# Group norm and quantised 3x3 convolution on one core: fewer plain images, no additions by hand in the middle, earlier input stores, a new timetable

## The chip, the core and the metric

The kernel runs on one core of one Trainium2 chip. The time is the device time of one execution in microseconds (us), and it is given as the median of several runs. A profile is one execution of its own, recorded by the hardware profiler; its times are read against that execution's time.

The core has five engines that run side by side, each with its own queue of instructions which it works off strictly in order: TensorE (PE, matrix products; its weight loads are listed as PEld), VectorE (DVE), ScalarE (ACT), GpSimd (POOL) and SyncE (SP), which here only issues DMAs. POOL issues DMAs too. 16 DMA engines carry the transfers of both queues. An instruction that needs another engine's result waits for a semaphore, and everything behind it on its own engine waits with it.

## What is computed

The input is 160 images of 128 channels and 32x32 pixels, with five sets of weights. Images are numbered here in the kernel's order, 32 per set.

```python
beta = jnp.max(U); alpha = jnp.min(U)
s1 = (beta - alpha) / 3.0
v1 = s1 * floor(U / s1)
s2 = s1 / 5.0
v2 = s2 * floor((U - v1) / s2)
w = (v1 + v2).reshape(128 * 5, 128, 3, 3)
...
x = x + conv3x3(group_norm(x, 32 groups), w)     # five groups, padding 1
```

So each image gets statistics (mean and variance of groups of four channels), is normalised, is convolved with its set's 3x3 weights, and the raw image is added to the result. The weights are quantised in two steps over the range of all five sets.

## The kernel before, in words

**Tiling.** The channels lie on the 128 partitions, an image is 1024 values of each. Two neighbouring images are a chunk; ten chunk places in SBUF hold loaded images (`CHUNKS`). A load brings a chunk (1 MB). A chunk's place can be loaded again once everything that reads its images is done.

**Two ways to convolve an image.** Both split the normalised image in a high and a low fp16 part, and PE multiplies both.

- A *plain* image (those in `PLAIN`, 33 of them) is normalised by POOL (`normalise_beside`, L858), ACT rounds it to the high part `hi` (L787), DVE subtracts for the low part `lo` (L894), and PE runs nine taps on two halves for two parts: 36 matmuls (L931).
- A *combined* image (120 of them) goes through sums and differences of pixels first. POOL (`differences`, L819 and L852) and DVE (`combine`, L831 and L838) write four quarters `v`; ACT scales and rounds them to `vh` (L881); DVE makes the rest `vl` (L887). PE then needs 24 matmuls (L986): six for each of two sums `m1` and `m2`, twelve for the two halves of the result. Between them ACT takes `m2` out of PSUM (`leave`, L1023), and DVE writes half the sum and half the difference of `m1` and `m2` into the two result banks (`pairs`, L1032 and L1034).

The images 0 to 6 are handled in ways of their own, which the change leaves alone.

**The result and the residual.** An image that is added *by hand* (`by_hand`: the first three, the last four and those in `HANDS`) is added to the raw image by DVE straight from PSUM (`residual`, L1075), and SP stores the sum (L1087); until then the image keeps its chunk place. For all others SP stores the raw image to the output early (`store_input`, L1094 for a whole chunk, L1087 for one image), ACT copies the result from PSUM to one of three `sum` buffers (the evacuation, L1058), and POOL issues a DMA that adds the buffer to what lies in the output (`accumulate`, L1081). That DMA waits for the store of the raw image, and the buffer is free when it has landed.

**Statistics.** Images are measured in groups of five. For most, ACT reads an image twice (`measure`: sum L377, squares L384); PE averages over channels; small instructions of DVE (L432 to L445), ACT (L415) and POOL (L422, a power) make `ngm`, `rstd`, `shift`.

**Weights.** While images of one set are convolved, the next set's weights are quantised in 42 small steps, most on DVE.

**What sets the order.** The first part (`run`) is written out by hand, with loads of chunks 1 to 9 ahead. From image 3 on (`steady`) the order on every queue is planned on the host by `Timetable`: each piece of work is a job with an engine, a cost in us, needs and a due time that is worked back from PE's list. `HASTE` moves due times by kind, `MARGIN` adds time after other engines' results, `SOON` says how long an engine is held free for an urgent job. Jobs with the engine "beside" are POOL's; they are placed beside `window` jobs of DVE (`pairs` and additions by hand), and then wait for DVE to get there. Stores and loads of SP are jobs of an endless queue with an assumed 14 us to landing. The plan fixes the order alone: on the chip each engine runs its list and waits where something is late.

Of the kernel before, what the change touches and what calls it, by code (L numbers as in the profile page):

```python
# [46 lines left out]
class Timetable:  # L47
# [6 lines left out]
    HOP = 0.14  # L54
    HASTE = {"combine": 5.0, "vh": -1.0, "vl": 1.0, "z": -5.0, "lo": 2.0, "sum": -3.0, "ve": -1.0, "power": -1.0, "scale": 2.0, "step": 1.0, "taps": -6.0, "across": 4.0}
    MARGIN = {"vh": 0.3, "pairs": 0.15, "hand": 0.45, "evac": 0.3, "t": 0.45}
    SOON = 0.6
    EARLY = 5.0
# [462 lines left out]
class Main:  # L521
# [24 lines left out]
    CHUNKS = 10  # L546
    LANDING = 14.0
    WIDE, HIGHS, ROWS, SUMS = 3, 4, 4, 3
    STEADY = 7
    BY_VECTOR = (8, 10, 11, 14, 19, 24, 29, 34)  # L550
    PLAIN = (9, 13, 17, *(22 + 9 * k + d for k in range(15) for d in (0, 4)))
    Z_ENGINE = "beside"
    HANDS = range(24, 156, 10)
    EARLY = 8
# [544 lines left out]
    def run(self):  # L1099
        nc, P = self.nc, self.P  # L1100
# [127 lines left out]
        for c in range(6, self.CHUNKS):  # L1228
            self.load(c)
        for i in range(self.FIRST):  # L1230
            j = (i - 1) % self.FIRST
            if i == self.FIRST - 1:
                for which in (1, 0):
                    self.sum_of_pairs(self.FIRST, which)
            self.direct_hi(j, self.COLS[2])
            self.direct_lo(j, self.COLS[2])
            if i == 0:
                self.stats[2].variances()
                self.stats[2].deviation()
                self.stats[2].power()  # L1240
                self.stats[2].scales()
                run(self.sums_across(0, nc.gpsimd))
                measure(0, 8, 9, 10)
            if i == 1:
                self.normalise(4)
                self.high_part(4)
            if i == 2:
                self.load_set(1)
                self.leave(3)
                self.normalise(5)  # L1250
                measure(1, 9)
                self.high_part(5)
                self.pairs(3)
                measure(0, 11)
                self.low_part(4)
                run(self.combinations(4))
            self.residual(j)
        self.steady(12, self.CHUNKS)

    def steady(self, measured, loaded):  # L1260
# [41 lines left out]
        for i in images:  # L1302
            comb, plain = self.combined(i), self.plain(i)
            if comb:
                beside[i] = add("t", "beside", 1.41, lambda i=i: self.differences(i))
                wide[i] = add("combine", "vector", 1.73, lambda i=i: self.combine(i))
                high[i] = add("vh", "scalar", 1.89, lambda i=i: self.high_combined(i), (beside[i], wide[i]))
                low[i] = add("vl", "vector", 2.28, lambda i=i: last_of(self.low_combined(i)), (high[i],))
            else:
# [21 lines left out]
            if i < imgs - 1:  # L1331
                out[i] = add("hand" if hand else "evac", "vector" if hand else "scalar", 1.15 if hand else 0.96, result, (main[i][1],))
                out[i].window = hand
            else:
                out[i] = add("hand", "vector", 2.0, result, (main[i][1],))
# [11 lines left out]
        for c in range(imgs // NB):  # L1347
            both, before = (range(k * NB, k * NB + NB) for k in (c, c - self.CHUNKS))
            if c >= loaded:
                loads[c] = add("load", "queue", self.LANDING, lambda c=c: self.load(c), (  # L1350
                    [stores.get(c - self.CHUNKS), *(j for i in before for j in readers(i))]
                ))
            if not all(self.by_hand(i) for i in both):
                stores[c] = add(
                    "store", "queue", self.LANDING, lambda c=c: self.store_input(c),
                    (loads.get(c), loads.get(c + 1)), ready=6.0 * c if c < loaded else 0.0,
                )
            for i in both:
                if not self.by_hand(i):
                    whole[i].after(stores[c])  # L1360

# [38 lines left out]
        for g, group in enumerate(self.groups):  # L1400
# [3 lines left out]
            for i in group:  # L1404
# [3 lines left out]
                if self.by_vector(i):  # L1408
# [3 lines left out]
                    continue  # L1412
                one = add("sum", "scalar", 1.06, lambda i=i: self.measure(i, (0,)), (load,))
                two = add("square", "scalar", 1.16, lambda i=i: self.measure(i, (1,)), (one,))
                measuring.append(two)
# [5 lines left out]
            ve = add("ve", "scalar", 0.16, lambda st=st: st.deviation(), (var,))  # L1421
            power = add("power", "beside", 0.4, lambda st=st: [st.power()], (ve,))
            scale = add("scale", "vector", 0.3, lambda st=st: st.scales_by_vector(), (power,))
            last_ve, last_dev = ve, dev
# [10 lines left out]
        for n in range(1, N_SETS):  # L1435
# [6 lines left out]
            for col in self.COLS:  # L1442
                gen = self.make_column(n, col, "later")
                for kind, cost in (
                    ("scalar", 0.7), ("vector", 0.74), ("vector", 0.56), ("vector", 0.56),
                    ("vector", 0.48), ("vector", 0.28), ("vector", 0.68), ("scalar", 0.5),
                    ("vector", 0.56), ("vector", 0.56), ("vector", 0.56), ("vector", 0.48),
                    ("vector", 0.28), ("vector", 0.5),
                ):
                    steps.append((kind, cost, gen))  # L1450
            taps = []
            for k, (kind, cost, gen) in enumerate(steps):
# [9 lines left out]
                if k % 14 == 13:  # L1462
# [3 lines left out]
                    taps.append(turned)  # L1466
            across = add("across", "vector", 0.9, lambda n=n: run(self.sums_across(n, nc.vector)), taps)
            for i in range(use, min(use + 3, imgs)):
# [66 lines left out]
```

## Time and profile before

| | before |
|---|---|
| median of 3 runs | 989.24 us (988.69 to 991.32) |
| the profiled execution, its own time | 988.58 us |
| its span, first to last instruction | 986.9 us |
| mean granted TensorE clock | 0.995 |
| PE, DVE, ACT, POOL busy | 937.3, 916.7, 854.2, 518.1 us |
| transfers | 246.88 MB, mean 250 GB/s |

The profile's page gives each engine's busy time; a table by stretches gives it for any part of the span, with the granted clock and the share of time in which the 16 DMA engines were moving packets (its highest value over ten microseconds is 1.05 in this trace). The waits list who idled for whom. A line such as L887 is a line of the kernel before; in the changed kernel, lines behind the first added one are one to four lines further down.

### The profile page before, as it was taken

Reading aid. Unit: us, or ns where it says so; the run is one execution under the profiler, and the core shown is the slowest. Engines: PE = TensorE matmul, PEld = TensorE weight load, DVE = VectorE, ACT = ScalarE, POOL = GpSimd, SP = SyncE. Lnnn points to the kernel's source line nnn. Section 1 sums busy time; section 2 is a strip of 40 time slices with the busy share of each in tenths; the row PEclk is TensorE's granted clock in tenths of the full one; section 3 lists DMA queues with packets and bytes.
Section 4 is the critical chain, followed back from the end, with each engine's and each line's share of the span. In section 5 each row is a group of like instructions: output and inputs, shape, how many; then the busy total and the mean of one; then the engine's idle time right before and its main releaser. Section 6 shows DMA issues by size and latency. Waiting matters only on the chain.

```text
span 986.9 us, 12939 instructions
## 1 busy us (share of the span) xinstructions
PE 937.3 (95%) x4514; PEld 442.6 (45%) x4514; DVE 916.7 (93%) x1175; ACT 854.2 (87%) x1118; POOL 518.1 (52%) x495
## 2 busy tenths in 40 slices
PE   2888998999999999999999999999999999999996
PEld 1433443444444444444444444444444444444443
DVE  7998897999999999999999999899999998978985
ACT  5786997979899899998999999899998999885551
POOL 4333454445555676655556655465645555556540
PEclk9999999999999999999999999999999999999999
DMA  9459999889999899999999799998989899874653
GB/s 357 188 176 387 322 325 331 252 198 316 246 280 264 221 317 257 305 237 289 252 274 283 196 320 269 297 259 258 309 199 317 223 274 276 217 123 85 95 92 118
DMA packets 65657, 246.88 MB, mean 250 GB/s; under 512 B 5296, under 2 KB 5296, under 8 KB 65584
## 3 DMA queue, kind: packets, MB, share of 16 engines
q1 hardware_dynamic: 45568, 173.09, 47.7%
q0 software_dynamic: 20016, 72.88, 39.7%
q8 instruction: 37, 0.61, 0.2%
q14 instruction: 36, 0.29, 0.1%
HBM read 89.19 MB, written 156.76 MB: 249 GB/s over the span
## 4 chain that ended last, share of the span: by engine, by line
PE 63%; DVE 19%; ACT 7%; DMA 5%; issue 4%; POOL 1%; SPq 0%; POOLq 0%; ACTq 0%; DVEq 0%
PE eo L986 22%; PE eo L931 18%; PE m L986 11%; PE m1b L986 5%; PE m1a L986 5%; DVE vl L887 5%; DMA xt<-in_x_dram 4%; DVE v L831 3%; ACT vh L881 2%; ACT junk L377 2%; DVE eo L1034 1%; DVE v L838 1%; DVE eo L1032 1%; DVE lo L894 1%; ACT junk L384 1%
## 5 line engine op out<-in xcount | busy, mean ns | idle before, releaser
L887 DVE SCALAR_TENSOR_TENSOR vl<-v,rstd,vh 128x2048 f16<-128x2048 f32 x120 | 290.6, 2423 | 26.4 <-ACT vh L881 26.1
L986 PE MATMUL eo<-vh,wt 128*128 128x512 f16 x720 | 269.6, 374 | 2.0 <-DVE eo L1034 2.0
L986 PE MATMUL eo<-vl,wt 128*128 128x512 f16 x720 | 269.6, 374 | 0.0
L881 ACT ACTIVATE vh<-v,rstd 128x2048 f16<-128x2048 f32 x120 | 239.0, 1996 | 21.5 <-DVE rstd L443 10.2
L819 POOL TENSOR_SCALAR v<-xt,ngm 128x64 f32<-128x64 f32 x120 | 127.9, 1065 | 199.4 <-issue 74.9
L986 PEld LDWEIGHTS <-across 128*128 128x128 f16 x1440 | 141.6, 98 | 179.1 <-issue 18.0
L986 PEld LDWEIGHTS <-wt 128*128 128x128 f16 x1488 | 145.1, 99 | 163.4 <-DVE eo L1034 1.8
L931 PEld LDWEIGHTS <-wt 128*128 128x128 f16 x1368 | 133.7, 99 | 155.1 <-DVE eo L1034 3.3
L931 PE MATMUL eo<-hi,wt 128*128 128x496 f16 (+3 forms) x702 | 185.6, 375 | 4.6 <-DVE eo L1034 2.6
L1058 ACT COPY sum<-eo 128x1024 f32<-128x1024 f32 x139 | 148.4, 1068 | 34.0 <-PE eo L986 18.4
L384 ACT ACTIVATE junk<-xt,mv 128x1024 uint8<-128x1024 f32 x152 | 174.5, 1148 | 2.8
L377 ACT ACTIVATE junk<-xt 128x1024 uint8<-128x1024 f32 x152 | 160.5, 1056 | 17.3 <-DMA xt<-in_x_dram 15.6
L931 PE MATMUL eo<-lo,wt 128*128 128x496 f16 (+2 forms) x630 | 166.6, 375 | 0.2 <-DVE lo L894 0.2
L1081 POOL DMA_DIRECT2D out_dram<-sum x139 | 122.7, 895 | 79.2 <-ACT sum L1058 74.5
L852 POOL TENSOR_TENSOR v<-xt 128x512 f32<-128x512 f32 x120 | 151.6, 1263 | 0.0
L986 PE MATMUL m<-vh,across 128*128 128x512 f16 x360 | 136.2, 378 | 9.4 <-ACT m L1023 9.4
L831 DVE TENSOR_TENSOR v<-xt 128x960 f32<-128x960 f32 x120 | 141.8, 1182 | 0.2
L986 PE MATMUL m<-vl,across 128*128 128x512 f16 x360 | 136.3, 379 | 2.6 <-DVE vl L887 2.5
L858 POOL TENSOR_SCALAR z<-xt,ngm,rstd 128x1024 f32<-128x1024 f32 x33 | 61.3, 1859 | 73.8 <-DVE vl L887 17.6
L1023 ACT ACTIVATE m<-m 128x512 f32<-128x512 f32 x124 | 73.5, 593 | 22.5 <-PE m L986 19.2
L838 DVE SCALAR_TENSOR_TENSOR v<-xt,twice 128x512 f32<-128x512 f32 x120 | 91.1, 759 | 0.0
L422 POOL TENSOR_TENSOR rstd<-ve,mhalf 128x5 f32<-128x5 f32 (+2 forms) x34 | 57.3, 1686 | 63.0 <-DVE v L831 28.1
(143 smaller groups left out, 993.6 us busy)
## 6 DMA issues: line engine op xcount, KB each, us to landing
xt<-in_x_dram SPq DMA_DIRECT2D x78, 1024.0 KB, 9.9
out_dram<-sum POOLq DMA_DIRECT2D x139, 512.0 KB, 8.8
out_dram<-xt SPq DMA_DIRECT2D x62, 1024.0 KB, 12.1
out_dram<-xt SPq DMA_DIRECT2D x35, 512.0 KB, 4.4
u<-in_L_conv_U_dram SPq DMA_DIRECT2D x4, 576.0 KB, 9.0
xt<-in_x_dram SPq DMA_DIRECT2D x4, 512.0 KB, 9.6
range<-in_L_conv_U_dram SPq DMA_DIRECT2D x3, 576.0 KB, 7.9
u<-in_L_conv_U_dram SPq DMA_DIRECT2D x2, 288.0 KB, 3.0
```

The costliest lines, as they stand in the source:

```text
L377: self.nc.scalar.activation(junk, image, ACTF.Copy, scale=-1.0 / image.shape[1], accum_out=self.mv[:, j, 0:1],)
L384: self.nc.scalar.activation(junk, image, ACTF.Square, bias=self.mv[:, j, 0:1], accum_out=self.mv[:, j, 1:2],)
L819: return self.nc.gpsimd.tensor_scalar(self.view(self.v[i], 0, (512 + W // 2 - 1, 2), (W // 2, H)), self.view(self.image(i), 1, (W - 3, 2), ...
L831: nc.vector.tensor_tensor(self.view(v, 1, (511, 2), (half, H), (1, half - 1)), self.view(x, 1, (1, 2), (W, H), (2, half - 1)), self.view(x ...
L838: nc.vector.scalar_tensor_tensor(v[:, 1024:1536], even, st.twice[:, j], odd, ALU.add, ALU.add)
L852: return [self.outer_columns(i), self.nc.gpsimd.tensor_sub(self.v[i][:, 1536:], odd, even)]
L881: self.nc.scalar.mul(vh, self.v[i], st.rstd[:, j])
L887: yield self.nc.vector.scalar_tensor_tensor(vl, self.v[i], st.rstd[:, j], self.hi[i], ALU.mult, ALU.subtract)
L931: nc.tensor.matmul(self.bank(target, a)[:, first:end, c0:c1], self.wts[n, col][:, k, :], tile[:, s0 : s0 + 2 * (end - first) - 1 : 2, c0 + ...
L986: self.nc.tensor.matmul(out, weights, moving, start=start and j == 0, stop=False, skip_group_check=True)
L1058: nc.scalar.copy(self.as_banks(i, self.sum[i]), self.flat(i, eo))
L1081: added = self.nc.gpsimd.dma_start(self.ov[n, :, b], self.sum.pop(i), accum_op=ALU.add)
```

## The change

- `PLAIN` has 28 images in place of 33: after 22 every fifth one up to 122, then 131, 139, 147 and 155. Five images thus become combined ones.
- `HANDS` is empty: 14 images (24, 34, ... 154) are no longer added by DVE, but evacuated by ACT and accumulated by a DMA of POOL.
- `STORED = 5`: the raw images of chunks 1 to 4 are stored right behind the first loads, in `run`, and are no jobs of the plan any more.
- A planned store of a chunk now needs the load of the second next chunk in place of the next one, and the early ones have other ready times.
- Constants of the plan change: `HASTE`, `MARGIN`, `SOON`, and the costs of several kinds of job.

```diff
-    HASTE = {"combine": 5.0, "vh": -1.0, "vl": 1.0, "z": -5.0, "lo": 2.0, "sum": -3.0, "ve": -1.0, "power": -1.0, "scale": 2.0, "step": 1.0, "taps": -6.0, "across": 4.0}
-    MARGIN = {"vh": 0.3, "pairs": 0.15, "hand": 0.45, "evac": 0.3, "t": 0.45}
-    SOON = 0.6
+    HASTE = {"t": 4.0, "combine": 3.0, "vh": 1.0, "vl": 2.0, "z": -4.0, "hi": 4.0, "lo": 2.0, "leave": -4.0, "pairs": 3.0, "hand": 17.0, "evac": -2.0, "sum": -4.0, "square": 6.0, "dev": -2.0, "ve": 4.0, "scale": 1.0, "step": -1.0, "taps": -14.0, "across": 5.0}
+    MARGIN = {"vh": 0.3, "vl": 0.3, "leave": 0.45, "pairs": 0.45, "hand": 0.45, "evac": 0.15, "t": 0.75}
+    SOON = 0.4
...
+    STORED = 5
...
-    PLAIN = (9, 13, 17, *(22 + 9 * k + d for k in range(15) for d in (0, 4)))
+    PLAIN = (9, 13, 17, *range(22, 126, 5), 131, 139, 147, 155)
     Z_ENGINE = "beside"
-    HANDS = range(24, 156, 10)
+    HANDS = ()
...
         for c in range(6, self.CHUNKS):
             self.load(c)
+        for c in range(1, self.STORED):
+            self.store_input(c)
...
-                wide[i] = add("combine", "vector", 1.73, lambda i=i: self.combine(i))
-                high[i] = add("vh", "scalar", 1.89, lambda i=i: self.high_combined(i), (beside[i], wide[i]))
-                low[i] = add("vl", "vector", 2.28, lambda i=i: last_of(self.low_combined(i)), (high[i],))
+                wide[i] = add("combine", "vector", 1.79, lambda i=i: self.combine(i))
+                high[i] = add("vh", "scalar", 1.9, lambda i=i: self.high_combined(i), (beside[i], wide[i]))
+                low[i] = add("vl", "vector", 2.30, lambda i=i: last_of(self.low_combined(i)), (high[i],))
...
-                out[i] = add("hand" if hand else "evac", "vector" if hand else "scalar", 1.15 if hand else 0.96, result, (main[i][1],))
+                out[i] = add("hand" if hand else "evac", "vector" if hand else "scalar", 1.15 if hand else 1.0, result, (main[i][1],))
...
-            if not all(self.by_hand(i) for i in both):
+            if c >= self.STORED and not all(self.by_hand(i) for i in both):
                 stores[c] = add(
                     "store", "queue", self.LANDING, lambda c=c: self.store_input(c),
-                    (loads.get(c), loads.get(c + 1)), ready=6.0 * c if c < loaded else 0.0,
+                    (loads.get(c), loads.get(c + 2)),
+                    ready=6.0 * (c - self.STORED + 1) if c < loaded else 0.0,
                 )
             for i in both:
                 if not self.by_hand(i):
-                    whole[i].after(stores[c])
+                    whole[i].after(stores.get(c))
...
-                one = add("sum", "scalar", 1.06, lambda i=i: self.measure(i, (0,)), (load,))
-                two = add("square", "scalar", 1.16, lambda i=i: self.measure(i, (1,)), (one,))
+                one = add("sum", "scalar", 1.09, lambda i=i: self.measure(i, (0,)), (load,))
+                two = add("square", "scalar", 1.21, lambda i=i: self.measure(i, (1,)), (one,))
...
-            power = add("power", "beside", 0.4, lambda st=st: [st.power()], (ve,))
-            scale = add("scale", "vector", 0.3, lambda st=st: st.scales_by_vector(), (power,))
+            power = add("power", "beside", 0.9, lambda st=st: [st.power()], (ve,))
+            scale = add("scale", "vector", 0.4, lambda st=st: st.scales_by_vector(), (power,))
...
-                    ("scalar", 0.7), ("vector", 0.74), ("vector", 0.56), ("vector", 0.56),
-                    ("vector", 0.48), ("vector", 0.28), ("vector", 0.68), ("scalar", 0.5),
-                    ("vector", 0.56), ("vector", 0.56), ("vector", 0.56), ("vector", 0.48),
-                    ("vector", 0.28), ("vector", 0.5),
+                    ("scalar", 0.71), ("vector", 0.66), ("vector", 0.57), ("vector", 0.54),
+                    ("vector", 0.57), ("vector", 0.38), ("vector", 0.67), ("scalar", 0.51),
+                    ("vector", 0.65), ("vector", 0.56), ("vector", 0.54), ("vector", 0.57),
+                    ("vector", 0.38), ("vector", 0.69),
...
-            across = add("across", "vector", 0.9, lambda n=n: run(self.sums_across(n, nc.vector)), taps)
+            across = add("across", "vector", 1.07, lambda n=n: run(self.sums_across(n, nc.vector)), taps)
```

## The prediction

> **What bounds the kernel now.** I read the busy table by stretches first, with one stretch from 220 us on, where PE has come to image 26, to 836 us, where it begins image 134.
>
> ```profile
> core 0: us, PE busy (x) PEld busy (x) DVE busy (x) ACT busy (x) POOL busy (x), PEclk, DMA share, GB/s
> 90.00:100.00 10.00, 5.09 (x26) 2.38 (x24) 4.51 (x5) 2.80 (x5) 3.86 (x5) 0.99 1.05 325
> 100.00:110.00 10.00, 10.00 (x41) 4.34 (x40) 8.68 (x8) 9.97 (x16) 3.62 (x5) 0.84 1.05 279
> 170.00:180.00 10.00, 6.77 (x26) 2.68 (x26) 9.84 (x13) 9.97 (x14) 3.20 (x5) 0.83 1.02 326
> 220.00:836.00 616.00, 614.25 (x2987) 292.13 (x2986) 597.03 (x732) 583.67 (x772) 355.93 (x310) 1.00 0.95 269
> 700.00:750.00 50.00, 50.00 (x246) 23.87 (x244) 48.83 (x64) 48.95 (x67) 26.84 (x25) 1.00 0.93 269
> 850.00:900.00 50.00, 50.00 (x243) 23.78 (x242) 41.09 (x51) 41.78 (x51) 25.34 (x25) 1.00 0.64 140
> 900.00:950.00 50.00, 50.00 (x238) 23.16 (x237) 45.63 (x43) 28.35 (x25) 30.60 (x28) 1.00 0.59 98
> ```
>
> In the middle PE is busy for 99.7% of 616 us: it is the bound, but DVE has 96.9%, ACT 94.8% and the DMA engines a share of 0.95. Behind 836 us PE is still full while DVE and ACT have room. The early stretch is another matter: PE idles and runs at a lower clock. So next the waits and, at 88 to 100 us, the instructions of POOL, ACT and PE in order of time.
>
> ```profile
> 87.53 1.22 POOL L858 TENSOR_SCALAR z<-xt,ngm,rstd 128x1024 f32<-128x1024 f32 x1 [5.28 <-DVE vl L887]
> 88.70 2.89 POOL L1081 DMA_DIRECT2D out_dram<-sum  x3
> ...
> 98.15 1.01 ACT L1058 COPY sum<-eo 128x1024 f32<-128x1024 f32 x1 [7.20 <-DMA out_dram<-sum]
> ...
> 99.71 0.50 PE L986 MATMUL m<-vh,across 128*128 128x512 f16 x1 [4.91 <-ACT m L1023]
> 100.00 0.63 PE L986 MATMUL m<-vl,across 128*128 128x512 f16 x1
> ```
>
> Three accumulates stood behind the z of a plain image, which itself waited 5.28 us. They left together at 88.70, all `sum` buffers were taken until one landed, ACT stood 7.20 us, PE 4.91, and the matmuls behind the gap lasted 0.63 us against the usual 0.37. The second early gap of PE (4.50 us, at 171 us) goes back to SP:
>
> ```profile
> SPq L1094 <- DMA xt<-in_x_dram: 228.3, 35, 13.6
> SPq L1087 <- DVE xt L1075: 195.1, 16, 56.5
> ```
>
> SP's stores stand in its queue until the chunk that they store has landed (total us, times, longest), and loads behind them stand too; stores of images added by hand do the same behind DVE. Last, the prices from the groups:
>
> ```profile
> L887 DVE SCALAR_TENSOR_TENSOR vl<-v,rstd,vh 128x2048 f16<-128x2048 f32 x120 | 290.6, 2423 | 26.4 <-ACT vh L881 26.1
> L1058 ACT COPY sum<-eo 128x1024 f32<-128x1024 f32 x139 | 148.4, 1068 | 34.0 <-PE eo L986 18.4 <-DMA out_dram<-sum 8.0 <-PE eo L931 3.8
> L1081 POOL DMA_DIRECT2D out_dram<-sum x139 | 122.7, 895 | 79.2 <-ACT sum L1058 74.5
> q0 software_dynamic: 20016, 72.88, 39.7%
> ```
>
> and from the chain in order of time a combined image's two halves and a plain image's whole (start, us):
>
> ```profile
> 593.32 2.54 PE eo L986 x12
> ...
> 606.00 7.62 PE eo L931 x36
> ```
>
> **The change, part by part.** The sum is made on the profiled execution: 988.58 us, of which the span is 986.9. The median of the runs is 0.66 above it.
>
> *PE.* A plain image takes PE 7.62 us (36 matmuls) and a combined one 2 x 2.54 = 5.08 (12 for the halves and 12 for m1 and m2). Up to image 25 both lists hold the same plain images, so all five that go lie behind 216 us, where PE is full: 24 against 21 of them in the images 26 to 133, 5 against 3 from 134 on. That is 3 x 2.54 = 7.6 us in the middle and 2 x 2.54 = 5.1 us in the end.
>
> *Whether DVE and ACT can follow in the middle.* DVE per image that becomes combined: + 1.182 (L831) + 0.759 (L838) + 2.423 (vl) + 0.694 + 0.699 (pairs) - 1.224 (lo) = 4.53 us over four more instructions. The rows overlap: in the middle they add up to 644 us where DVE was busy 597, or 0.065 us for each of 732 instructions, so 4.27 us. An addition by hand is 1.22 - 0.065 = 1.155. Three images more and ten hands fewer: 12.8 - 11.6 = + 1.3, to 598.3 us. ACT, with an overlap of 0.071 worked out likewise: per such image + 1.995 (vh) + 0.592 (leave) - 1.041 (hi) = 1.546, less 0.071 = 1.475; per hand that becomes an evacuation 1.069 - 0.071 = 1.0. 4.4 + 10.0 = + 14.4, to 598.1 us. PE would like 616 - 7.6 = 608.4 us, so both would have to be 98.3% full. The fullest 50 us with PE at 50.00 are 700 to 750, with 97.7% and 97.9%; at their mean of 97.8% the middle lasts 611.7 us, so 3.3 us come back. The bounds are 0 (all fit) and + 22.6 (ACT gets no fuller than the 94.8% of this middle: 598.1 / 0.948 = 631). I take 3.3, because that row is nearest to the state asked for, and PE's 50.00 in it shows that nobody waited.
>
> *The end.* The two plain images and three hands change DVE by + 8.5 - 3.5 us and ACT by + 3 + 3 over 138 us in which they have 9 and 8 us in 50 to spare at the least full (850 to 900) and DVE 4.4 (900 to 950). Hidden; the 5.1 us of PE count fully. Without that cover up to 5 us would return.
>
> *The first gap.* The changed order on POOL puts the accumulates of images 3 and 4 ahead of that z, and the raw images they wait for are stored behind the first loads. In the row of 40 to 50 us the DMA share is 0.01, so these stores (3.67 MB; the hardware queue moved 173.09 MB in 47.7% of the span, 2.72 us per MB, so 10 us) fill a hole. On SP the four stand behind the loads of chunks 6 to 9, ahead of the stores of images 0 to 2 and the second set's weights; they wait for chunks that have landed by then, so they hold nothing up. I take the whole gap: 4.91 us, and 10 x (1 - 0.84) = 1.6 for the clock, together - 6.5. What is late next is the second gap.
>
> *The second gap and SP.* The 10 us of stores leave the stretch from 70 to 180 us where the share is 1.02 to 1.05. Against that, the load of chunk 14 is moved past eight stores, one of which waits for chunk 13 to land (longest such wait 13.6 us); loads 15 and 16 stand behind it, and ACT's statistics of images 28 to 33 wait for these. The pair of loads 18 and 19 stands behind stores of 16 and 17 in both orders. So from - 8 (4.50 + 0.42 + 1.35 + 1.7 for the clock, all gone) to + 13.6; I take 0, since 10 us of stores taken out and 6.5 us mean of such a wait (228.3 / 35) nearly cancel. The 14 waits of SP behind hands (16 waits, 195 us before) go; no PE wait hangs on them, so they are costed at nothing, and the load they delay is covered by 16 to 18 images of lead of ACT's reading over its evacuation.
>
> *DMA.* An accumulate takes 39.7% x 986.9 / 139 = 2.82 us of all 16 engines; the raw store replaces the store of the sum. Ten more in the middle: 0.95 x 616 + 28.2 = 613 us in 608, a share of 1.01 under the 1.05 seen at most. Nothing on the mean, but see the rivals.
>
> *POOL.* Fourteen more accumulates of 0.9 us, each behind a wait for ACT (74.5 / 37 = 2 us where there was one), with the next v and z behind them, which feed vh on ACT: 40 us on an engine that is idle for 469 of 987. Nothing, up to + 6: in the middle the means of L831, L838, L887 and the scale (L443) stand 24 us above their medians (a vl of 2.35 us lasts up to 3.51), and a quarter more of that is what fewer additions by hand beside POOL's work could cost.
>
> The Trainium skill speaks against this part: "GPSIMD Engine Reference", the specifications, has GpSimd share its SBUF interfaces with VectorE and contend with Vector instructions that have two SBUF inputs. An addition by hand reads PSUM and one SBUF input, and lasts 1.216 to 1.228 us here whatever POOL does; L831 and L887 read two and do stretch, which agrees. By the rule the sum would be up to 6 us higher; by the rows' means, which hold the stretching already, it is unchanged.
>
> Sum: 988.6 - 7.6 + 3.3 - 5.1 - 6.5 = 972.7; with 0.66 for the median, **973 us**.
>
> **The rivals.**
>
> *The second gap closes too* (12%). For it: 10 us fewer stores before it. Against: the same store in front of the load. 973 - 8 = 965 us.
>
> *ACT and DVE give the middle's gain back* (13%): ACT at 96.2%, the mean of 97.8 and 94.8, lasts 621.7, 10 more than assumed: 983 us; spread to 992. For it: three engines near their ends at once. Against: 700 to 750 us.
>
> *The loads come late: slower* (17%). Place: ACT's first reading of a chunk, in the middle. With a share of 1.01 the queues have little to catch up with, a load lands later than ACT's turn to read it, and ACT, PE and then everything stand, as from 70 to 180 us, where with the share at 1.02 to 1.05 PE lost about 16 us in 110. If a third of the middle (200 us) runs so, + 30: 1003 us. It is slower than before from 22 us on, that is when ACT gets no fuller than 95%. For it: loads took 22.5 us there, against a median of 9.9. Against: here the demand stays under 1.05, and there ten chunks had to be caught up.
>
> *The change doesn't do what it says*: excluded, the order of the changed kernel has 125 vl, 28 z and 153 accumulates.
>
> **How the numbers follow.** The forecast, 966 to 984, has 58%. The measurement can tell about 0.3%, 986.3 to 992.2. Faster: 58 + 12 + 5 of the give-back = 75%; same: the other 8%; slower: 17%. The range 962 to 991 leaves out the slow case and little else.
>
> **What would show it.** PE near 100% from 220 us on and 12.7 us less busy in total; DVE and ACT both at 97 to 98% in the middle, DMA share about 1.00; no ACT wait for out_dram<-sum near 90 us; the gap at 171 us still there. I am wrong if ACT's reading (L377) waits for loads for more than 20 us, or if vh waits for POOL grow from 5.8 us to tens.

## The result and the profile after

| | before | after |
|---|---|---|
| median | 989.77 us (988.69 to 991.41) | 989.63 us (987.95 to 992.18) |
| ratio of after to before | | 1.0, 95% interval 0.9991 to 1.0009 |
| the profiled execution's own time | 988.58 us | 989.55 us |
| its span | 986.9 us | 987.8 us |
| PE busy, matmuls | 937.3 us, 4514 | 928.1 us, 4454 |
| PE idle in the span | 49.6 us | 59.7 us |
| DVE busy | 916.7 us | 949.1 us |
| ACT, POOL busy | 854.2, 518.1 us | 870.2, 506.4 us |

The change makes no difference that can be measured, where 973 us was forecast. PE has 60 matmuls less to do and yet the end comes at the same time. The page of after, first the busy times and then the shares of the chain that ended last:

```profile
PE 928.1 (94%) x4454; PEld 432.7 (44%) x4454; DVE 949.1 (96%) x1181; ACT 870.2 (88%) x1137; POOL 506.4 (51%) x514
...
DVE 52%; PE 27%; issue 10%; ACT 5%; DMA 3%; POOL 1%; DVEq 0%; ACTq 0%; POOLq 0%; SPq 0%
```

The same line of the chain in before:

```profile
PE 63%; DVE 19%; ACT 7%; DMA 5%; issue 4%; POOL 1%; SPq 0%; POOLq 0%; ACTq 0%; DVEq 0%
```

By this chain the bound has gone over from PE to DVE. Where in time this happens is in the table by stretches (columns as in the prediction: length, then PE, weight loads, DVE, ACT, POOL busy with their instructions, clock, DMA share, GB/s). Before, in two stretches not shown yet:

```profile
60.00:220.00 160.00, 141.78 (x666) 65.39 (x665) 142.72 (x207) 138.01 (x187) 68.51 (x68) 0.98 0.95 294
...
836.00:960.00 124.00, 123.80 (x593) 58.04 (x592) 109.27 (x117) 88.42 (x94) 67.77 (x64) 1.00 0.63 128
```

After:

```profile
90.00:100.00 10.00, 10.00 (x49) 4.60 (x48) 9.77 (x17) 9.92 (x14) 8.27 (x8) 1.00 1.04 348
100.00:110.00 10.00, 10.00 (x51) 4.79 (x49) 9.90 (x17) 9.50 (x12) 2.59 (x4) 1.00 1.04 325
170.00:180.00 10.00, 9.81 (x49) 4.62 (x47) 9.93 (x10) 9.92 (x16) 5.58 (x6) 1.00 1.04 304
60.00:220.00 160.00, 150.34 (x722) 69.83 (x721) 157.63 (x220) 152.84 (x207) 74.31 (x75) 1.00 1.01 310
220.00:836.00 616.00, 595.95 (x2868) 277.48 (x2867) 605.71 (x717) 575.51 (x754) 323.06 (x318) 1.00 0.98 269
350.00:400.00 50.00, 45.80 (x221) 21.00 (x220) 49.67 (x54) 45.00 (x57) 24.63 (x25) 1.00 0.92 247
650.00:700.00 50.00, 50.00 (x243) 23.52 (x242) 49.52 (x60) 48.02 (x64) 24.94 (x28) 1.00 1.03 295
836.00:960.00 124.00, 123.70 (x594) 57.93 (x592) 122.40 (x128) 99.91 (x111) 82.38 (x67) 1.00 0.70 136
```

Read PE's idle time as length less busy. From 60 to 220 us it falls from 18.2 to 9.7 us: both early gaps are closed, and the clock stands at 1.00 where it was 0.84 and 0.83. From 220 to 836 us it rises from 1.7 to 20.1 us. The account closes: busy time - 9.2, idle early - 8.6 and in the middle + 18.3, elsewhere + 0.4, together + 0.9 us, which is what the spans differ by. In the middle DVE is busy 605.71 of 616 us, 98.3%, and in 350 to 400 us 49.67 of 50 while PE has 45.80. The waits of PE there, in after (total us, times, longest):

```profile
PE eo L987 <- DVE eo L1035: 12.6, 18, 1.7
PE m L987 <- ACT m L1024: 3.7, 3, 2.5
PE m L987 <- DVE vl L888: 1.8, 3, 0.9
```

No wait is long; PE is held up a little, often, for DVE's `pairs`. The same can be followed by the end of the pairs of an image, counted off in order in both traces: image 28 comes 11.5 us earlier than before (219.1 against 230.6), image 79 at the same time (520.8 and 520.9), image 129 7.9 us later (815.3 and 807.4), and from there to 159 after takes 160.8 us against 168.1. So the two ends meet by chance: a lead of 11.5 us, a loss of 19.4 and a gain of 7.3 happen to add up to nothing.

DVE's 949.1 us are more than its instructions explain. The prediction's prices give 5 x 4.27 - 14 x 1.155 = + 5.2 us; measured + 32.4. The groups of DVE (name, shapes, times, busy us, mean ns, idle before) tell which. Before:

```profile
L831 DVE TENSOR_TENSOR v<-xt 128x960 f32<-128x960 f32 x120 | 141.8, 1182 | 0.2
L838 DVE SCALAR_TENSOR_TENSOR v<-xt,twice 128x512 f32<-128x512 f32 x120 | 91.1, 759 | 0.0
L894 DVE TENSOR_TENSOR lo<-z,hi 128x1024 f16<-128x1024 f32 x40 | 49.0, 1224 | 0.0
```

After:

```profile
L832 DVE TENSOR_TENSOR v<-xt 128x960 f32<-128x960 f32 x125 | 158.2, 1266 | 0.3 <-POOL v L820 0.3
L839 DVE SCALAR_TENSOR_TENSOR v<-xt,twice 128x512 f32<-128x512 f32 x125 | 103.2, 826 | 0.0
L895 DVE TENSOR_TENSOR lo<-z,hi 128x1024 f16<-128x1024 f32 x35 | 54.6, 1559 | 0.0
L1035 DVE SCALAR_TENSOR_TENSOR eo<-m1b,m 128x512 f32<-128x512 f32 x65 | 45.4, 699 | 2.2
```

The same work on the same tiles lasts longer in the mean, while the pairs, which read PSUM, keep the 699 ns that they had. In the runs below this is put in one number, the *stretching*: for every DVE instruction the time above the tenth percentile of its form, added up. It is 52.5 us before and 84.4 us after; without it the durations add up to 933.8 and 937.2 us, so the work itself grew by 3.4. `combine` and `lo` carry most of the growth (L831 from 4.0 to 15.0 us, L838 from 2.5 to 11.1, `lo` from 0.5 to 12.0), while the scale of the statistics (L443) falls from 17.5 to 1.9. In the middle alone the stretching is 38.9 and 61.0 us. Nearly all of it lies on instructions that had a POOL instruction running beside them, 50.0 of the 52.5 us before and 82.1 of the 84.4 after, and each of the 73 instructions of after that lasted over 0.2 us more than the tenth percentile of its form had one. In order of time it looks like this, DVE and POOL of after (start, duration):

```profile
377.53 2.34 DVE L888 SCALAR_TENSOR_TENSOR vl<-v,rstd,vh 128x2048 f16<-128x2048 f32 x1
...
377.83 2.29 POOL L820 TENSOR_SCALAR v<-xt,ngm 128x64 f32<-128x64 f32 x1
...
379.79 1.87 DVE L300 SCALAR_TENSOR_TENSOR rest<-k,s1n,u 128x384 f32<-128x384 f16 x1
...
380.09 1.03 POOL L853 TENSOR_TENSOR v<-xt 128x512 f32<-128x512 f32 x1
```

A `rest` lasts 0.742 us in the median and here 1.87, with POOL's 1.03 us subtraction inside it; POOL's L820, which takes 0.37 us at the least, lasts 2.29 beside a `vl`. In these lines one stands while the other works.

### The profile page after: what moved, and what is told of

The parts are those of the page before. It is cut to its first block, busy times and chain, and to the rows that moved or that the text cites. A ratio compares the mean times of both kernels' runs of the same rounds, so it can differ in the third digit from the quotient of the medians.

```text
span 987.8 us, 12937 instructions
## 1 busy us (share of the span) xinstructions
PE 928.1 (94%) x4454; PEld 432.7 (44%) x4454; DVE 949.1 (96%) x1181; ACT 870.2 (88%) x1137; POOL 506.4 (51%) x514
## 4 chain that ended last, share of the span: by engine, by line
DVE 52%; PE 27%; issue 10%; ACT 5%; DMA 3%; POOL 1%; DVEq 0%; ACTq 0%; POOLq 0%; SPq 0%
DVE vl L888 14%; PE eo L987 10%; DVE v L832 9%; PE eo L932 7%; DVE v L839 6%; DVE eo L1033 5%; PE m L987 5%; DVE eo L1035 4%; DVE lo L895 3%; PE m1b L987 2%; PE m1a L987 2%; DMA out_dram<-sum 2%; DVE tt L284 1%; DVE tt L282 1%; ACT vh L882 1%
## 5 line engine op out<-in xcount | busy, mean ns | idle before, releaser
L888 DVE SCALAR_TENSOR_TENSOR vl<-v,rstd,vh 128x2048 f16<-128x2048 f32 x125 | 304.0, 2433 | 1.0 <-ACT vh L882 0.9
L987 PE MATMUL eo<-vh,wt 128*128 128x512 f16 x750 | 281.1, 375 | 19.0 <-DVE eo L1035 18.3
L987 PE MATMUL eo<-vl,wt 128*128 128x512 f16 x750 | 280.8, 374 | 0.0
L820 POOL TENSOR_SCALAR v<-xt,ngm 128x64 f32<-128x64 f32 x125 | 120.0, 960 | 221.3 <-DVE v L832 53.1
L987 PEld LDWEIGHTS <-wt 128*128 128x128 f16 x1548 | 148.1, 100 | 192.3 <-DVE eo L1035 38.0
L1059 ACT COPY sum<-eo 128x1024 f32<-128x1024 f32 x153 | 163.6, 1069 | 37.2 <-PE eo L987 14.7
L1082 POOL DMA_DIRECT2D out_dram<-sum x153 | 136.0, 928 | 84.1 <-ACT sum L1059 74.6
L932 PEld LDWEIGHTS <-wt 128*128 128x128 f16 x1188 | 115.8, 98 | 136.9 <-DVE eo L1035 3.5
L377 ACT ACTIVATE junk<-xt 128x1024 uint8<-128x1024 f32 x152 | 160.6, 1057 | 10.9 <-DMA xt<-in_x_dram 9.6
L932 PE MATMUL eo<-hi,wt 128*128 128x496 f16 (+2 forms) x612 | 161.8, 375 | 3.1 <-DVE eo L1035 2.2
L832 DVE TENSOR_TENSOR v<-xt 128x960 f32<-128x960 f32 x125 | 158.2, 1266 | 0.3 <-POOL v L820 0.3
L932 PE MATMUL eo<-lo,wt 128*128 128x512 f16 (+1 forms) x540 | 142.6, 375 | 0.3 <-DVE lo L895 0.2
L839 DVE SCALAR_TENSOR_TENSOR v<-xt,twice 128x512 f32<-128x512 f32 x125 | 103.2, 826 | 0.0
L422 POOL TENSOR_TENSOR rstd<-ve,mhalf 128x5 f32<-128x5 f32 (+2 forms) x34 | 55.6, 1637 | 63.5 <-DVE v L832 44.3
L859 POOL TENSOR_SCALAR z<-xt,ngm,rstd 128x1024 f32<-128x1024 f32 x28 | 56.0, 2000 | 59.0 <-DVE dv L438 27.5
```

What stands on the lines that cost most here:

```text
L377: self.nc.scalar.activation(junk, image, ACTF.Copy, scale=-1.0 / image.shape[1], accum_out=self.mv[:, j, 0:1],)
L820: return self.nc.gpsimd.tensor_scalar(self.view(self.v[i], 0, (512 + W // 2 - 1, 2), (W // 2, H)), self.view(self.image(i), 1, (W - 3, 2), ...
L832: nc.vector.tensor_tensor(self.view(v, 1, (511, 2), (half, H), (1, half - 1)), self.view(x, 1, (1, 2), (W, H), (2, half - 1)), self.view(x ...
L839: nc.vector.scalar_tensor_tensor(v[:, 1024:1536], even, st.twice[:, j], odd, ALU.add, ALU.add)
L888: yield self.nc.vector.scalar_tensor_tensor(vl, self.v[i], st.rstd[:, j], self.hi[i], ALU.mult, ALU.subtract)
L932: nc.tensor.matmul(self.bank(target, a)[:, first:end, c0:c1], self.wts[n, col][:, k, :], tile[:, s0 : s0 + 2 * (end - first) - 1 : 2, c0 + ...
```

## The experiments

The edits are to the kernel before or to the changed kernel, as said. "Middle" is the busy time of PE and DVE from 220 to 836 us of the profile. Gains and losses between kernels are taken from these ratios, times 989.5 us.

| kernel | median, us | ratio to before, 95% | DVE busy | stretching | middle: PE, DVE |
|---|---|---|---|---|---|
| after | 989.63 | 0.9991 to 1.0009 | 949.1 | 84.4 | 595.95, 605.71 |
| a1_hands | 998.46 | 1.0082 to 1.0109 | 920.7 | 73.1 | 610.88, 598.47 |
| a2_plain | 990.65 | 1.0005 to 1.0024 | 929.4 | 45.9 | 607.91, 601.25 |
| a3_stored | 979.59 | 0.9884 to 0.9915 | 917.1 | 54.1 | 613.99, 596.26 |
| a4_plan | 993.99 | 1.0027 to 1.0054 | 924.1 | 60.5 | 612.66, 600.00 |
| f1_no_added | 997.43 | 1.0061 to 1.0088 | 920.1 | 73.0 | 610.95, 598.99 |
| e1_hands_back | 999.86 | 1.0083 to 1.0114 | 960.2 | 78.7 | 588.19, 602.77 |
| c2_less | 962.23 | 0.9709 to 0.9736 | 890.7 | 21.3 | 612.94, 582.52 |
| c3_less_before | 988.75 | 0.9975 to 0.9993 | 881.7 | 14.0 | 615.35, 573.13 |
| b1_oldplan | 989.29 | 0.9996 to 1.002 | 923.2 | 55.5 | 606.26, 594.87 |
| g1_less_oldplan | 975.12 | 0.9844 to 0.9873 | 885.1 | 14.0 | 612.05, 574.94 |
| g2_dve_less | 972.38 | 0.9817 to 0.9843 | 918.8 | 84.9 | 604.56, 593.84 |
| g3_dve_less_oldplan | 983.19 | 0.992 to 0.9943 | 898.2 | 61.5 | 608.50, 578.31 |
| b2_oldplain | 985.79 | 0.9943 to 0.9969 | 914.2 | 66.8 | 612.58, 595.35 |
| e2_tail | 975.50 | 0.9848 to 0.988 | 923.9 | 53.3 | 613.71, 597.63 |
| n1_hop | 992.04 | 1.0019 to 1.0043 | 918.8 | 55.6 | 612.72, 596.19 |
| n2_hop | 988.34 | 0.9985 to 1.0003 | 909.4 | 45.4 | 615.01, 590.25 |

**One part of the change alone.** Four kernels, each the kernel before with one part of the change and nothing else. No addition by hand in the middle:

```diff
-    HANDS = range(24, 156, 10)
+    HANDS = ()
```

> The kernel before with HANDS empty and nothing else changed: 14 additions leave VectorE, 14 evacuations go to ScalarE, 14 accumulates to the DMA engines. Vector theory (VectorE became the bound of the changed kernel): VectorE's busy time falls by about 16 us to some 901, TensorE stays the bound, so 985 to 991 us. Transfer theory (the 39 us of accumulates, which bring the DMA share near 1.0, cost the gain): 995 us or more, with ScalarE waiting for loads. If the windows lost with the additions stretch VectorE, its busy time falls by less than 8 us.

The new list of plain images:

```diff
-    PLAIN = (9, 13, 17, *(22 + 9 * k + d for k in range(15) for d in (0, 4)))
+    PLAIN = (9, 13, 17, *range(22, 126, 5), 131, 139, 147, 155)
```

> The kernel before with the new list of 28 plain images alone: TensorE's busy time falls by 12.7 us, VectorE gets 5 x 4.27 = 21 us more. Vector theory: VectorE at 938 us or more becomes the bound, 988 to 998 us, and TensorE waits for its pairs. Transfer theory: the transfers are those of before, so most of the 12.7 us is gained, 977 to 981 us.

The early stores, with the new need and ready time of the planned ones:

```diff
+        for c in range(1, self.STORED):
+            self.store_input(c)
```

> The kernel before with the early stores and the changed needs of the planned stores alone. All theories: the early gaps near 99 and 171 us shrink and TensorE reaches image 28 some 8 to 11 us earlier. If TensorE then stays the bound, that lead lasts to the end: 978 to 982 us. If VectorE is already so full at the old balance that it eats the lead, 986 to 990 us.

The constants of the plan and the costs of the jobs (`HASTE`, `MARGIN`, `SOON`):

```diff
-    SOON = 0.6
+    SOON = 0.4
...
-            power = add("power", "beside", 0.4, lambda st=st: [st.power()], (ve,))
+            power = add("power", "beside", 0.9, lambda st=st: [st.power()], (ve,))
```

> The kernel before with the new constants of the plan alone (due-time shifts, margins, the hold for urgent jobs, job costs); all work is the same. Plan theory (the new order puts GpSimd's work beside VectorE's two-input instructions): VectorE's busy time rises by 15 us or more over 917, and the time to 990 us or more. Vector theory without that (the stretching comes from VectorE being the bound): busy time within 6 us of before and 984 to 990 us.

Measured: + 9.5, + 1.4, - 9.9 and + 4.1 us, in sum + 5.1, where all together give none. Only the early stores gain. The list alone gains nothing although PE has 60 matmuls less: DVE goes from 597.03 to 601.25 us of the middle, 97.6%, and PE idles 8.1 us in it. The constants take DVE's busy time up by 7 us and the stretching to 60.5; a change of order that means nothing (n2_hop below) moves DVE's busy time by as much, downwards. The empty `HANDS` alone costs time, and DVE's busy time rises by 4 us where 16 should go: the stretching rises by 20.6 us, to 73.1, more than the additions took away. In a1_hands the gap of PE at 171 us, 4.50 us before, is 8.39 us:

```profile
175.48 0.59 PE L986 MATMUL m<-vh,across 128*128 128x512 f16 x1 [8.39 <-ACT m L1023]
```

and the clock of 170 to 180 us is 0.53 (before 0.83). ACT, for which PE waits there, has itself waited for a load before it reads the next chunk (L377). Before and in a1_hands:

```profile
165.71 1.06 ACT L377 ACTIVATE junk<-xt 128x1024 uint8<-128x1024 f32 x1 [6.02 <-DMA xt<-in_x_dram]
...
169.72 1.06 ACT L377 ACTIVATE junk<-xt 128x1024 uint8<-128x1024 f32 x1 [9.94 <-DMA xt<-in_x_dram]
```

SP issues that load at 150.04 us before and at 153.54 in a1_hands, in both behind the store of a raw image or chunk that has to wait for an earlier load. An image added by hand has no such store, only one of its sum later on; the empty list brings fourteen more of them, two of them between 70 and 180 us, where the DMA share is 1.02 to 1.05, and the loads land later. This makes the added stores the likely reason; no run tests it. This gap and 3.4 us less PE work in the middle are where the loss of a1_hands lies.

**Whether the added transfers do it.** As a1_hands, but the fourteen new accumulating DMAs are not issued; those images keep the raw input as their output. The order on DVE, ACT and PE is that of a1_hands.

```diff
+        if i in range(24, 156, 10):
+            self.sum.pop(i)
+            return
```

> The kernel before with HANDS empty, but the accumulating DMAs of those 14 images are not issued (their output stays the raw input); the order of VectorE, ScalarE and TensorE is the same as with HANDS empty. Transfer theory (the 39 us of accumulates cost the 9 us that HANDS empty lost): back to 991 us or less, with an early gap near 175 us as short as before. Window theory (without the additions GpSimd's work runs beside VectorE's other instructions): 995 us or more, VectorE's busy time near 921 as with HANDS empty.

997.43 us: 2 us less than a1_hands, with intervals that overlap. The accumulating transfers are not the cause. The raw stores of the fourteen images are still issued here, and ACT's reading waits 11.33 us for the same load (PE is busy for 1.79 us of 170 to 180), so this run does not clear those. DVE's busy time and stretching are those of a1_hands, as the window theory had it.

**Additions by hand in the changed kernel.** The same part, undone in the changed kernel:

```diff
-    HANDS = ()
+    HANDS = range(24, 156, 10)
```

> The changed kernel with the 14 additions by hand of the kernel before. Taken alone, empty HANDS cost 9 us, the plain list 1, the plan's constants 4.5, and the early stores gained 10. If the parts add up: 980 to 983 us, and VectorE's busy time stays within 8 us of 949 although it has 16 us more work, since the stretching goes. If the plan's constants had been fitted to empty HANDS: 987 us or more.

+ 9.7 us over after, with DVE's busy time + 11.1. So the empty list, which costs 9.5 us in the kernel before, is worth 9.7 in the changed one, where no reading of ACT waits for a load after 15 us. The parts can't be added up.

**GpSimd's work beside DVE.** In the changed kernel POOL's subtraction writes 32 of 512 columns of a quarter; the others keep zeros (the `v` buffers are three fixed ones, cleared once, so that these can be read). Everything else is issued as before.

```diff
-        return [self.outer_columns(i), self.nc.gpsimd.tensor_sub(self.v[i][:, 1536:], odd, even)]
+        return [self.outer_columns(i), self.nc.gpsimd.tensor_sub(self.v[i][:, 1536:1568], odd[:, :32], even[:, :32])]
```

> The changed kernel with GpSimd's subtraction for a combined image done on 32 of 512 columns (the rest of that quarter keeps old values, so the results are not the reference's); order and VectorE's instructions are the same. It takes some 1 us of GpSimd's work from each of 125 images. Stretching theory (VectorE bounds the changed kernel, and more than it should because GpSimd's work beside it stretches its two-input instructions): VectorE's busy time falls from 949 by 20 us or more and the time to 970 to 980 us. Rival (VectorE's instructions are stretched by something else, or its load alone without stretching is too much): busy time falls by less than 8 us and the time stays at 985 us or more.

The same cut in the kernel before:

> The same cut of GpSimd's work in the kernel before. Stretching theory: TensorE bounds it, and little of VectorE's stretching comes from there, so VectorE's busy time falls by 5 to 15 us and the time by less than 4 us (985 to 990). Rival (the kernel before was as much bound by stretched VectorE work as the changed one): 980 us or less.

DVE was not given less to do in either, and is busy 58.4 and 35.0 us less: the stretching goes from 84.4 to 21.3 and from 52.5 to 14.0. In time this is worth 27.5 us after and 1.6 us before. The time of c2_less is below its expected 970 to 980 us, and DVE's fall in c3_less_before is more than twice the expected 5 to 15 us; what was expected of its time came true. The middle of c2_less:

```profile
220.00:836.00 616.00, 612.94 (x2974) 290.40 (x2973) 582.52 (x739) 594.40 (x779) 287.23 (x330) 1.00 1.00 279
```

and of c3_less_before:

```profile
220.00:836.00 616.00, 615.35 (x2995) 293.00 (x2994) 573.13 (x738) 585.80 (x772) 289.54 (x313) 1.00 0.96 270
```

PE is full in both. Before, the stretching lay beside PE's bound and cost next to nothing; after, it lies on the engine that sets the end. But c2_less also makes POOL's result come earlier, so the next run leaves POOL alone.

**DVE's own work, and the plan.** In the changed kernel DVE's second operation of `combine` writes 256 of 512 columns (the others keep zeros), and POOL is left alone:

```diff
-            v[:, 1024:1536], even, st.twice[:, j], odd, ALU.add, ALU.add
+            v[:, 1024:1280], even[:, :256], st.twice[:, j], odd[:, :256], ALU.add, ALU.add
```

> The changed kernel with VectorE's sum of pixels for a combined image done on 256 of 512 columns (results not the reference's); GpSimd's work is untouched. It takes 0.27 us from each of 125 images, 33 us of VectorE's own work. Vector theory (its total, with the stretching, is the bound): busy time 949 - 33 or a little more, time 960 to 970 us, as with GpSimd's cut. Latency rival (GpSimd in the chain is what counted): 980 us or more.

DVE - 30.3 us, the stretching unchanged (84.9), the time 972.38: - 16.8. That is nearer to the 960 to 970 us of a DVE that sets the end than to no change, and missed it by 2.4. PE still idles 11.4 us in the middle, with DVE at 96.4% of it. So less work on DVE, with POOL's left as it was, is worth at least this much; whether by its load or because a shorter `combine` also lets `vh` start earlier, this run doesn't tell. For each us off DVE's busy time it brings 0.55 us, and c2_less 0.47: the larger cut explains the larger gain, and POOL's earlier result need not have brought anything. Little waits for it in after, as the wait of `vh` shows:

```profile
ACT vh L882 <- POOL v L820: 2.7, 2, 2.1
```

A path round about isn't excluded: POOL issues the accumulates, and ACT's waits for a `sum` buffer fall from 13.5 us in after to 2.3 in c2_less. Nor is there a run with the three fixed buffers and nothing cut.

The changed kernel with the old constants and costs of the plan (a4_plan backwards):

> The changed kernel with the constants of the plan of the kernel before (due-time shifts, margins, hold, job costs); the 28 plain images, empty HANDS and early stores stay. Plan theory (the new constants make the order in which GpSimd's work lies beside VectorE's two-input instructions): VectorE's busy time falls from 949 by 12 us or more and the time to 975 to 984 us. Load theory (any order of so full a VectorE leaves GpSimd's work no other place): busy time within 8 us of 949 and 986 us or more.

and the two cuts in this kernel, POOL's and DVE's:

> The changed kernel with the old constants of the plan, and GpSimd's subtraction on 32 of 512 columns (results not the reference's). With the old constants VectorE is not stretched (923 us) and the time is 989 all the same. If GpSimd's place in the chain to an image's high part (its latency) holds it: 965 to 976 us. If the old order itself holds it, whatever GpSimd costs: 982 us or more.

> The same cut of VectorE's work with the old constants of the plan. If VectorE's load holds that version too: 965 to 976 us. If the old order holds it, with no engine full: 982 us or more.

With the other three parts in place, the constants make the stretching: with the old ones DVE is busy 923.2 us, 26 less, and stretched 55.5. But the time doesn't move: the median is 989.29 us, in runs from 986.85 to 995.2. The middle of b1_oldplan and the waits of PE from 200 to 960 us, in the fastest of them:

```profile
220.00:836.00 616.00, 606.26 (x2938) 286.57 (x2937) 594.87 (x728) 580.58 (x747) 375.12 (x325) 1.00 0.99 278
```

```profile
PE eo L987 <- DVE eo L1035: 8.2, 5, 3.6
PE m L987 <- DVE vl L888: 6.9, 5, 2.7
PE m L987 <- ACT m L1024: 2.3, 3, 1.6
```

Here DVE has room (96.6%), and PE loses its time in a few long waits in place of many short ones, from places where the old plan's order lets `vl` and the pairs come late. This order answers less to either cut: g3_dve_less_oldplan gains 7.5 us for 25.0 us of DVE's busy time and g1_less_oldplan 14.8 for 38.1, or 0.30 and 0.39 for each. PE idles 9.7 us in the middle and 4.9 from 836 to 960 us; after loses more in the middle and nothing there.

**Plain images.** The changed kernel with the 33 plain images of before:

```diff
-    PLAIN = (9, 13, 17, *range(22, 126, 5), 131, 139, 147, 155)
+    PLAIN = (9, 13, 17, *(22 + 9 * k + d for k in range(15) for d in (0, 4)))
```

> The changed kernel with the 33 plain images of the kernel before. Stretching theory: VectorE is relieved of 21 us and more, falls to 930 us or less, TensorE (plus 12.7 us) bounds again, and with the early gaps closed the time is that of the early stores alone, 977 to 983 us. Rival (what VectorE loses is not its load): 987 us or more.

985.79 us, 4.4 less than after, DVE 914.2 and PE's idle time in the middle 3.4 us: more matmuls and a kernel that is, if anything, faster. The time lies 2.8 us above the upper end of what was expected. And the kernel before with the early stores and plain images fewer at the end only, where DVE had room:

```diff
-    PLAIN = (9, 13, 17, *(22 + 9 * k + d for k in range(15) for d in (0, 4)))
+    PLAIN = (9, 13, 17, *(22 + 9 * k + d for k in range(12) for d in (0, 4)), 131, 139, 147, 155)
```

> The kernel before with the early stores and, of the new plain list, only its end: 131, 139, 147, 155 in place of 130, 134, 139, 143, 148, 152 (31 plain images), hands and plan as before. Behind image 126 VectorE has room, so TensorE's 5.1 us count: 979.6 - 5.1 = 972 to 976 us. If VectorE fills up there as it did in the changed kernel: 979 us or more.

975.50 us, the fastest kernel that leaves nothing out, and faster than both. Its middle and part of its end:

```profile
220.00:836.00 616.00, 613.71 (x2979) 291.36 (x2978) 597.63 (x728) 583.60 (x765) 356.23 (x311) 1.00 0.95 267
...
836.00:960.00 124.00, 122.81 (x588) 57.44 (x587) 117.30 (x126) 86.52 (x95) 70.64 (x62) 1.00 0.65 123
```

DVE is at 97.0% in the middle, as before, and at 94.6% in the end, and PE is busy for 99.6 and 99.0% of them. By the ratios it is 0.0036, 3.6 us, under a3_stored; two plain images fewer at the end were priced at 5.1. A difference of this size is one that another order can make, as the next runs show.

**How much an order moves by itself.** The kernel before with the plan's time for a signal between engines (`HOP`, 0.14) at 0.15 and at 0.13; the work is the same.

> The kernel before with one constant of the plan nudged (the added time for another engine's result, 0.14 to 0.15 us), which changes no work and means nothing on the chip. It sizes what another order alone does: if the order's luck is small, 988 to 991 us; if it is as large as the single parts measured (1 to 9 us), 985 or less or 994 or more.

> The kernel before with the same constant of the plan nudged the other way, 0.14 to 0.13 us. The first nudge cost 0.3%. If another order is mostly worse than the one that the constants were chosen for: 990 to 994 us; if it is luck to both sides: 985 to 989 us as likely.

+ 0.31% and - 0.06%. A change of order that means nothing can cost 3 us. The + 1.4 us of a2_plain are no more than that, and the + 4.1 of a4_plan, the - 4.4 of b2_oldplain and the - 3.6 of e2_tail little more; the - 9.9 of the early stores, the + 9.5 and + 9.7 of the additions by hand and the effects of the cuts are far above it.

## Why the prediction was wrong, and where it was right

*PE (- 12.7 us in total):* right in direction. 60 matmuls went; the busy time fell by 9.2 us. Why not by 12.7 stays open.

*The first gap (- 6.5 us):* right. 90 to 110 us is full in after, at a clock of 1.00, with ACT busy for 9.92 and 9.50 us; all its waits for a `sum` buffer in the whole run come to 13.5 us, the longest 2.9. Either part that the prediction named is nearly enough by itself: PE is busy for 20.00 of these 20 us with the early stores alone (a3_stored) and for 19.67 with the constants alone (a4_plan).

*The second gap (0, bounds - 8 to + 13.6):* the lower half was true, as the first rival had it. 170 to 180 us goes from 6.77 to 9.81 us of PE at full clock. The gap began with ACT's wait of 6.02 us for a load, and in after no reading of ACT waits for a load behind the first 15 us: the loads come in time although they stand behind the stores. Early stores alone brought 9.9 us of time, of 14.5 that both gaps were priced at.

*The end (- 5.1 us, hidden on DVE and ACT):* right. From image 129 on after gains 7.3 us on before.

*Whether DVE and ACT can follow in the middle (+ 1.3 us for DVE, 3.3 us back):* this is the step that failed, together with the line on POOL (nothing, up to + 6). Between images 28 and 129 after loses 19.4 us (11.5 + 7.9) where it was to gain 4.3. Two things were wrong in it. First, the price of DVE's instructions was taken from the means of before and held fixed, while it depends on what POOL does beside them: the stretching grew by 31.9 us over the whole run and by 22.1 in the middle, nearly four times the bound of 6. Second, 97.8% was read off 50 us with PE full as a level at which nobody waits; in a2_plain, with little stretching (45.9 us) and DVE at 97.6% of the whole middle, PE idles 8.1 us there, as much as the 7.6 that the three plain images were worth. A level reached over 50 us is not one that an order keeps up for 616. Nor does the level by itself say what is lost: PE idles 1.7 us at 96.9% of DVE before, and 11.4 us at 96.4% in g2_dve_less.

That the lost time in the middle hangs on DVE's instructions is shown from three sides: PE's waits name it, taking the stretching away (c2_less) fills PE again, and taking DVE's own work away without touching POOL (g2_dve_less) brings 16.8 us. Whether it is DVE's load or the moment at which its results come isn't told apart. The stretching comes from the order and from no single part: the new constants are 29 us of it in the changed kernel (b1_oldplan) and 8 in the kernel before (a4_plan), and the empty `HANDS` alone adds 21 there (a1_hands). That the stretching is the *only* reason for the missing gain is not so: with the stretching down to 55.5 us in b1_oldplan, the old order loses as much in long waits.

The rule that spoke against this change in the prediction ("GPSIMD Engine Reference", the specifications, of the Trainium skill: GpSimd and VectorE contend for SBUF where a Vector instruction has two SBUF inputs) was the right one to weigh. The runs agree with it: `combine` and `lo` stretch, the pairs that read PSUM stay at 692 and 699 ns. Its growth in this kernel is 32 us, 22 of them in the middle, not 6.

*The rivals.* "ACT and DVE give the middle's gain back" (13%, 983 us, spread to 992) is what happened, further than its 983 us and by DVE alone; ACT has room, 575.51 of 616 us. "The loads come late" (17%) did not: ACT's reading waits for loads 9.6 us in 2 waits, both in the first 15 us, the bound set was 20, and a DMA share of 1.03 in 650 to 700 us goes with PE at 50.00. What the prediction asked to see of DVE, 97 to 98% in the middle, was there at 98.3, as the sign of a limit and not of a fit. And neither of its two signs of being wrong came: besides the loads, `vh`'s waits for POOL fell from 5.8 to 2.7 us. The signs watch the loads and POOL's lateness; the lengthening of DVE's own instructions, which the line on POOL names and puts at nothing, has none.

Open: whether the added raw stores make the load late that a1_hands waits for; and whether DVE costs the time in the middle by its load or by when its results come.

## What to carry to other kernels

Moving work between engines that all stand above 95% is priced by what will run beside it, not by its mean in the old order: look at how far an instruction's mean lies above its median and which engine runs meanwhile, and treat that difference as something that the move can change; here the stretching went from 52.5 to 84.4 us. Measure the parts of a mixed change one by one, and in the new surroundings too, for the same part cost 9.5 us in one and saved 9.7 in the other. Here the part that paid was the early stores, and the work saved on the bounding engine showed nothing in the middle, where a helper was full, while the end, where its helpers had room, came 7.3 us shorter.

## What the runs showed of the hardware that was not expected

- In the lines above VectorE and GpSimd instructions on SBUF hold one another up for about the other's length: a `rest` of 0.742 us in the median lasted 1.87 with a GpSimd subtraction of 1.03 inside it, a GpSimd column operation of 0.37 us at the least lasted 2.29 beside a `vl` of 2.34. "Trainium Architecture — The Big Picture" of the Trainium skill (section "What this means for kernel authors") calls the pair of ports that the two share an exclusive lock and not a split of bandwidth, and these lines agree. It hits tiny instructions too: the scale of five columns (L443) has a mean of 0.811 us before and 0.286 after, and all 11 of the 28 before that lasted 0.2 us or more beyond the tenth percentile had a GpSimd instruction beside them.
- It is a cost that shows as busy time: in the kernel before, VectorE was busy 35 us less with the same work (c3_less_before), and that was worth 1.6 us.
- A DMA share of 1.03 over 50 us took nothing from PE, and fourteen accumulating transfers left out changed 2 us, with intervals that overlap (f1_no_added against a1_hands).
